# Graph layer on one core: the first four nodes' last 3456 edges counted instead of gathered

## The chip, the cores and the metric

The kernel runs on one core of a Trainium2 chip. TensorE (PE) multiplies, VectorE (DVE) and ScalarE (ACT) work elementwise, GpSimd (POOL) issues the indirect DMAs here (gathers and scatters by lists of rows), and SyncE (SP) and ACT issue plain DMAs. The metric is device time in microseconds, the median of several executions. The profile is of one execution.

## The reference

A layer on 3125 nodes with 256 features and 100000 edges, sorted by destination. `x` is normalized by rows; then the graph part, a linear-attention part and a mixture of experts follow:

```python
xn = _layernorm(x, axis=-1)
# graph part
e = relu((xn[dst] - xn[src]) @ theta_w.T + theta_b + xn[src] @ phi_w.T + phi_b)
gnn = segment_max(e, dst)              # 0 for a node without edges
# attention part: q, instance-normalized k and v, out = q (k^T v) / N, projected
x = x + gnn + mix(xn)
# experts: layernorm, router, two of eight experts (256 -> 1024 -> 256), weighted
x = x + ffn(_layernorm(x))
```

For a node d with edges, the maximum over edges of relu(a[d] + b[s]) is relu(a[d] + max b[s]), where a = xn theta^T + biases and b = xn (phi - theta)^T. So the graph part needs, for each node, the largest row b[s] over the sources s of its edges, feature by feature. An edge that occurs twice counts as once. The destinations are distributed as the square of a uniform number: low nodes have very many edges (node 0 has 1747), high nodes few.

## The kernel before

Nodes are cut into 25 tiles of 128 rows. Everything is done in the order of falling node numbers, so the edge lists are handed over reversed, with 96 filler edges (destination -1) at the end. 100096 edges are 782 columns of 128.

**Stages.** (1) All tiles are normalized, and b is computed and stored in DRAM as `b_d`. (2) The edges are worked through in four groups of columns, `GROUPS` and `STEPS` (lines 41 and 42): 240 columns for tiles 12 to 24, 161 for tiles 6 to 11, 228 for tiles 1 to 5, and 153 for tile 0 alone. One indirect DMA per column gathers 128 rows of `b_d` (line 1283, issued by the helper at line 102). Each of the 128 partitions holds a contiguous run of edges, so a running maximum along the columns, one DVE operation per column (`fold`, line 358), gives the maximum of every node that ends in the run; `cut` resets it where the destination changes. Windows of eight columns are stored to `s_d`. (3) When a group's columns are done, `carry` (line 361) passes maxima from one partition to the next with two transposes, a scan and two transposes back, and the tiles of the group are routed (`token_tile`, line 414): gather the last row of each node from `s_d`, add what is carried over, the linear parts, normalize, compute router scores, take the best two. `dispatch` scatters the tiles' rows into expert order (`xs_d`, line 109). (4) `Stream` (line 641) runs the experts for groups 0, 1 and 2 in units of 256 rows: first matmul (line 602), Gelu (line 604), second matmul (line 628), bias matmul (line 727); the results go to `ys_d`. (5) Tile 0, the last to be complete, isn't scattered: `dense_tile` (line 761) runs all eight experts on its 128 rows and weighs them. Its scaled inputs are made on DVE (line 777). (6) `combine` (line 1188) gathers each routed row's two results (48 gathers), weighs them (line 1201) and stores the output.

While the edges are gathered, the attention part (`mixer`, line 945) and the search for each node's last edge (`places`, line 282) run beside.

**What sets the order.** The order on PE, DVE, ACT and SP is the order in which the program writes the instructions (`manual_schedule`, line 828). A small planner in the program decides it: tasks are generators that yield how many ticks they wait; the clock `now` advances by one with each indirect DMA (lines 1010 to 1017 and 1284), and `on_pe` estimates PE's time so that the stream's steps are written as PE will need them. So a tick is about one POOL gather. A fold is written six ticks (`LAG`) after its gather, but for the very last columns, when no gather follows, at once (line 1246). DMAs on SP and ACT keep the order in which they are written. In this clock, group 1 is handed to the stream at tick 527; group 2's last fold is at tick 691, its scatters at 734 and 742, and it is handed over at 748; the edges end at 854, and the stream's end is estimated for 859.

**The end.** Group 3 (tile 0) begins its carry only when the stream has been written to its end:

```python
        while g == G - 1 and g - 1 not in at_hand["ffn"].through:
            yield 0.5
        start(carry(at_hand["tok"], mm, g, clock["last"], chain, carried))
```

The last six columns of group 3 aren't stored and gathered again, but picked by matmuls with one-hot columns (`pick_ends`, line 1176). Tile 0 uses ACT's Sqrt, then loads the Gelu table (line 465).

Before the end, `order` (line 895) checks that the edges are sorted and that each group holds only its nodes; if not, `verdict` sends the kernel to a general path behind line 1300, which doesn't run for these inputs.

## Time and profile before

| | |
|---|---|
| median of five runs | 1258.58 us (1247.89 to 1261.13) |
| the profiled execution | 1251.14 us, span 1249.1 us |
| busy: PE, DVE, ACT, POOL | 953.8, 651.1, 330.5, 910.2 us |
| edge gathers on POOL | 782, 762.0 us busy, 245.3 us idle before them |
| folds on DVE | 778, mean 484 ns |
| result gathers (`ys_d`) | 48 |
| last edge gather starts | 1148.0 us |
| stream's last matmul ends | 1150.2 us |
| dense tile, first to last matmul | 1171.6 to 1242.6 us |

The page shows one execution. Its slices cut the span into 40 parts of 31 us; a digit is a tenth of busy time. A group's line gives the busy time, the mean of one instruction, and the idle time of the engine before them with what ended most of it; "issue" is time in which nothing that the profile shows was waited for. In the timeline a row is start, duration, engine, line, operation, operands, and in brackets the wait before it.

### The profile page before, as it was taken

Reading aid. Unit: us, or ns where it says so; the run is one execution under the profiler, and the core shown is the slowest. Engines: PE = TensorE matmul, PEld = TensorE weight load, DVE = VectorE, ACT = ScalarE, POOL = GpSimd, SP = SyncE. Lnnn points to the kernel's source line nnn. Section 1 sums busy time; section 2 is a strip of 40 time slices with the busy share of each in tenths; the row PEclk is TensorE's granted clock in tenths of the full one; section 3 lists DMA queues with packets and bytes.
Section 4 is the critical chain, followed back from the end, with each engine's and each line's share of the span. In section 5 each row is a group of like instructions: output and inputs, shape, how many; then the busy total and the mean of one; then the engine's idle time right before and its main releaser. Section 6 shows DMA issues by size and latency. Waiting matters only on the chain.

```text
span 1249.1 us, 13251 instructions
## 1 busy us (share of the span) xinstructions
PE 953.8 (76%) x3894; PEld 686.9 (55%) x3894; DVE 651.1 (52%) x1931; ACT 330.5 (26%) x759; POOL 910.2 (73%) x938
## 2 busy tenths in 40 slices
PE   6548777739504469699999999999974449999777
PEld 5324333324202234288887888888862338886666
DVE  7668767863347663333348553333337833433632
ACT  4212222211101231133333333333310113332322
POOL 6677777777777777777777677777777777777751
PEclk9778988869855557799999999999995559999789
DMA  8669877676766654578877688999995669998581
GB/s 281 205 206 316 305 230 239 231 233 204 268 223 236 231 172 135 201 236 298 314 256 265 213 302 316 310 351 360 359 347 173 207 220 369 404 363 291 196 309 58
DMA packets 103276, 325.89 MB, mean 261 GB/s; under 512 B 20534, under 2 KB 41519, under 8 KB 91802
## 3 DMA queue, kind: packets, MB, share of 16 engines
q0 software_dynamic: 45328, 123.27, 32.0%
q1 hardware_dynamic: 26428, 115.34, 23.4%
q10 hardware_dynamic: 31438, 86.33, 19.6%
q8 instruction: 33, 0.54, 0.2%
q14 instruction: 49, 0.40, 0.1%
HBM read 192.97 MB, written 131.89 MB: 260 GB/s over the span
## 4 chain that ended last, share of the span: by engine, by line
PE 27%; DMA 25%; POOL 24%; issue 13%; DVE 10%; ACT 1%; POOLq 0%; DVEq 0%; SPq 0%; ACTq 0%
POOL g L102 23%; DMA g<-b_d,srcI 21%; PE hp L602 9%; PE yp L628 8%; DVE g L358 3%; DMA r<-s_d,end_i 2%; PE bp L234 2%; PE mm L395 2%; PE yp L727 1%; PE mm L393 1%; PE am L437 1%; POOL xs_d L109 1%; DVE r L442 1%; PE tr L227 1%; DVE r L443 1%
## 5 line engine op out<-in xcount | busy, mean ns | idle before, releaser
L102 POOL DMA_INDIRECT g<-b_d,srcI x782 | 762.0, 974 | 245.3 <-issue 214.2
L358 DVE SCALAR_TENSOR_TENSOR g<-g,cut 128x256 f32<-128x256 f32 x778 | 376.6, 484 | 425.0 <-DMA g<-b_d,srcI 409.9
L602 PE MATMUL hp<-xe,w 128*128 128x256 f32 (+1 forms) x1216 | 300.3, 373 | 12.0 <-issue 8.5
L628 PE MATMUL yp<-w,hT 128*128 128x256 f32 x1120 | 292.3, 383 | 0.0
L602 PEld LDWEIGHTS hp<-xe,w 128*128 128x128 f32 x1216 | 221.5, 195 | 51.5 <-issue 18.5
L604 ACT ACTIVATE hT<-hp,sm 128x256 f32<-128x256 f32 (+1 forms) x320 | 144.8, 453 | 336.2 <-PE hp L602 333.7
L628 PEld LDWEIGHTS yp<-w,hT 128*128 128x128 f32 x1120 | 207.5, 191 | 36.7 <-issue 11.0
L949 PE MATMUL kv<-wkv,xn_hi 128*128 128x512 f32 x104 | 60.8, 739 | 29.9 <-DVE kn L967 29.1
L949 PE MATMUL kv<-wkv,xn_lo 128*128 128x512 f32 x96 | 52.7, 700 | 36.7 <-DVE kn L967 22.6
L437 PE MATMUL am<-cr,oh 128*128 128x257 f32 x88 | 40.1, 590 | 42.9 <-DVE r L442 39.6
L102 POOL DMA_INDIRECT g<-ys_d,from_i x48 | 46.5, 968 | 27.4 <-issue 12.2
L949 PEld LDWEIGHTS kv<-wkv,xn_hi 128*128 128x128 f32 x104 | 23.5, 237 | 58.6 <-issue 52.7
L949 PEld LDWEIGHTS kv<-wkv,xn_lo 128*128 128x128 f32 x96 | 20.5, 225 | 61.3 <-issue 57.8
L437 PEld LDWEIGHTS am<-cr,oh 128*128 128x128 f32 x88 | 22.1, 284 | 52.8 <-issue 42.0
L727 PE MATMUL yp<-b_sb,ident 8*128 8x256 f32 x128 | 44.4, 426 | 0.0
L393 PE MATMUL mm<-bias,ones 1*128 1x512 f32 x50 | 31.8, 719 | 14.3 <-ACT x_sb L400 11.1
L953 ACT ACTIVATE sq<-kv 128x1024 f32<-128x1024 f32 x25 | 25.5, 1022 | 58.7 <-PE kv L949 58.7
L686 ACT ACTIVATE xe<-trf,sm 128x256 f32<-128x256 f32 x64 | 32.5, 561 | 21.3 <-PE trf L677 21.3
L972 PEld LDWEIGHTS dots_p<-kn,vn 128*128 128x128 f32 x200 | 26.8, 197 | 20.0 <-issue 20.0
L961 ACT ACTIVATE rsk<-var,eps 128x16 f32<-128x16 f32 x25 | 7.7, 308 | 110.0 <-DVE var L958 110.0
L109 POOL DMA_INDIRECT xs_d<-xn_hi,slot_i x26 | 27.1, 1043 | 9.9 <-issue 8.1
L972 PE MATMUL dots_p<-kn,vn 128*128 128x128 f32 x200 | 27.4, 282 | 8.7 <-DVE kn L967 8.7
(264 smaller groups left out, 947.5 us busy)
## 6 DMA issues: line engine op xcount, KB each, us to landing
s_d<-g SPq DMA_DIRECT2D x79, 1024.0 KB, 5.0
w<-in_w ACTq DMA_DIRECT2D x84, 512.0 KB, 7.0
s_d<-g SPq DMA_DIRECT2D x18, 896.0 KB, 4.3
g<-b_d,srcI POOLq DMA_INDIRECT x782, 4.3
w<-in_w ACTq DMA_DIRECT2D x6, 2048.0 KB, 9.6
xn_hi<-xs_d ACTq DMA_DIRECT2D x16, 512.0 KB, 4.5
xs_d<-zero ACTq DMA_DIRECT2D x8, 512.0 KB, 6.3
xs_d<-zero ACTq DMA_DIRECT2D x16, 256.0 KB, 3.3
```

The source lines that it names most:

```text
L102: got = nc.gpsimd.indirect_dma_start(out=to, out_offset=None, in_=table, in_offset=row_index(index))
L109: put.append(nc.gpsimd.indirect_dma_start(out=table, out_offset=row_index(index), in_=of, in_offset=None))
L358: nc.vector.scalar_tensor_tensor(g[:, j, :], last, cut[:, t:t + 1], g[:, j, :], op0=OP.add, op1=OP.max)
L393: nc.tensor.matmul(am, ones[0:1, :], bias, start=True, stop=False)
L437: nc.tensor.matmul(r2, picks[k], carried[g], start=(k == 0), stop=(k == len(slices) - 1))
L602: nc.tensor.matmul(hp[:, 0:n], w1t[:, c, f, :], xe[:, c, 0:n], start=(c == 0), stop=(c == 1))
L604: nc.scalar.activation(hT[f][:, 0:n], hp[:, 0:n], AF.Gelu, bias=sm[:, 4 + f, e:e + 1])
L628: nc.tensor.matmul(yp[r], hT[q][:, r * P:(r + 1) * P], w2t[:, q, :], start=(q == 0), stop=(q == FC - 1 and self.whole))
L686: nc.scalar.activation(xe[:, c, :], self.held["tr", u][:, c, :], AF.Identity, bias=sm[:, 2 + c, e:e + 1], scale=sm[:, c, e:e + 1])
L727: nc.tensor.matmul(yp, ident[0:E, e:e + 1].to_broadcast([E, P]), b2_sb, start=False, stop=True)
L949: nc.tensor.matmul(kv[:, k, :], xnT(i, c), wkv[:, c, k * INNER:(k + 1) * INNER], start=(c == 0), stop=(c == 1))
L972: nc.tensor.matmul(dots_p[:, r, :], vn[:, r * P:(r + 1) * P], knf[:, r * P:(r + 1) * P], start=(i == 0 and r == 0), stop=(i == NT - 1), sk ...
```

## The change

The last 27 columns (3456 edges, 96 of them filler) are taken out of group 3, which has 126 columns left; they belong to nodes 0 to 3 alone. For these columns `first_nodes` counts, by bf16 matmuls of one-hot matrices, how often each of the 3125 nodes is a source of an edge to each of the four nodes, and turns the counts into a mask: 0 where there is an edge, -1e38 where there is none. It is written early, between `borders` and `places`. `first_maxima` then reads the whole of `b_d` again, one 128x256 tile after the other on SP's queue, and takes for each of the four nodes max(b + mask) on DVE: 100 operations of 128x256, one per two ticks, begun when group 1 is handed to the stream. Transposes and a reduction bring the maximum over the partitions; tile 0's routing takes it in with one more maximum on four rows.

Further: the carry of group 3 no longer waits until the stream is written to its end; instead the dense tile waits for that after its transposes and before its first scaling. Tile 0 takes its roots on DVE (`newton=True`) instead of by ACT's Sqrt, and two table loads are dropped. The indices of the 27 columns are loaded by two DMAs of their own, the sortedness check knows a fifth slice, and a last edge beyond the gathered columns now gives "no row" instead of the last gathered row.

```diff
-STEPS = (240, 161, 228, 153)
+STEPS = (240, 161, 228, 126)
+FIRST = 4
+REST = T - COL[G]
...
-            nc.vector.tensor_scalar(end_i[:, i0:i1], has[:, i0:i1], float(most), None, op0=OP.min)
+            nc.vector.scalar_tensor_tensor(end_i[:, i0:i1], has[:, i0:i1], float(most), has[:, i0:i1], op0=OP.is_le,
+                                           op1=OP.mult)
...
             nc.vector.tensor_max(r1, r1, also["rows"])
+            nc.vector.tensor_max(r1[0:FIRST, :], r1[0:FIRST, :], also["first"])
...
         if then:
-            nc.scalar.activation(table, eps, AF.Gelu)
...
             clock["through"] = True
-            nc.scalar.activation(table, eps, AF.Sqrt)
...
+        while ready is not None and "through" not in ready:
+            yield 1
         scaled(0)
...
-        while ready is not None and "through" not in ready:
-            yield 1
         units = Units(ps, act, P, True)
...
-    for g in range(G):
-        move(nc.sync, srcI[:, COL[g]:COL[g + 1]], rows_of(src, g))
-        move(nc.sync, dstI[:, COL[g]:COL[g + 1]], rows_of(dst, g))
+    for g in range(G + 1):
+        of_slice = slice(COL[g], COL[g + 1] if g < G else T)
+        move(nc.sync, srcI[:, of_slice], rows_of(src, g))
+        move(nc.sync, dstI[:, of_slice], rows_of(dst, g))
...
         yield from borders(ea, mm, firsts, lasts, ok, following)
+        yield 4
+        yield from first_nodes()
         yield 80
         yield from places(ea, mm, run, keys, [(GROUPS[g], P * COL[g + 1]) for g in range(G)], following)
+    def first_nodes():
...
+        counts = no_edge.rearrange("p k i -> p (k i)")
+        some = 7
+        for t0 in range(0, REST, some):
+            n = min(some, REST - t0)
+            ones_of = []
+            for name, at, width in (("lanes", low, P), ("tiles", high, FIRST * NT)):
+                ones_of.append(ea.tile([P, some, width], BF16, name=name))
+                nc.vector.tensor_tensor(ones_of[-1][:, 0:n, :], apart[:, None, 0:width].to_broadcast([P, n, width]),
+                                        at[:, t0:t0 + n, None].to_broadcast([P, n, width]), OP.is_equal)
+                yield 2
+            count_p = mm.tile([P, FIRST * NT], F32, name="mm")
+            for t in range(n):
+                nc.tensor.matmul(count_p, ones_of[0][:, t, :], ones_of[1][:, t, :], start=(t == 0), stop=(t == n - 1))
+            yield 3
...
+        nc.vector.tensor_scalar(counts, counts, 0.5, NEG, op0=OP.is_lt, op1=OP.mult)
...
-        while g == G - 1 and g - 1 not in at_hand["ffn"].through:
-            yield 0.5
         start(carry(at_hand["tok"], mm, g, clock["last"], chain, carried))
...
-                              then=lambda: start(dense), also=ends))
+                              newton=True, then=lambda: start(dense), also=ends))
...
+        if g == 1:
+            start(first_maxima())
...
+    def first_maxima():
+
+        i0 = GROUPS[1][0]
+        of_k = xn_lo[:, i0:i0 + FIRST, :]
+        b_rows = b_d.rearrange("(i p) d -> p i d", p=P)
+
+        def bring(i):
+            if i < NT:
+                move(nc.sync, xn_lo[:, SPLIT - 2 + i % 2, :], b_rows[:, i, :])
+
+        bring(0)
+        yield 8
+        for i in range(NT):
+            bring(i + 1)
+            b = xn_lo[:, SPLIT - 2 + i % 2, :]
+            for k in range(FIRST):
+                if i == 0:
+                    nc.vector.tensor_scalar(of_k[:, k, :], b, no_edge[:, k, 0:1], None, op0=OP.add)
+                else:
+                    nc.vector.scalar_tensor_tensor(of_k[:, k, :], b, no_edge[:, k, i:i + 1], of_k[:, k, :], op0=OP.add,
+                                                   op1=OP.max)
+                yield 2
+        most = at_hand["first"].tile([P, 2, FIRST], F32, name="most")
+        for c in range(2):
+            tr = mm.tile([P, FIRST, P], F32, name="mm")
+            for k in range(FIRST):
+                nc.tensor.transpose(tr[:, k, :], of_k[:, k, c * P:(c + 1) * P], ident)
+            on_pe(1.2)
+            yield 4
+            nc.vector.tensor_reduce(most[:, c, :], tr, AX.X, OP.max)
+            yield 2
+        rows_p = mm.tile([FIRST, 2, P], F32, name="mm")
+        for c in range(2):
+            nc.tensor.transpose(rows_p[:, c, :], most[:, c, :], ident)
...
-                    while clock["edges"] < min(COL[g] + t0 + j + LAG, T):
+                    while clock["edges"] < min(COL[g] + t0 + j + LAG, COL[G]):
```

## The prediction

> **What bounds the kernel now.** First the page's slices, then the table of stretches, then the time order of the last 100 us.
>
> ```profile
> PE   6548777739504469699999999999974449999777
> ...
> POOL 6677777777777777777777677777777777777751
> ...
> PEclk9778988869855557799999999999995559999789
> ...
> L102 POOL DMA_INDIRECT g<-b_d,srcI x782 | 762.0, 974 | 245.3 <-issue 214.2
> ```
>
> POOL is evenly busy from the first gather to slice 37: one gather each 1.29 us (762.0 + 245.3 over 782) and almost no waits. PE is full in slices 17 to 29 (expert stream, groups 0 and 1), drops for three slices at half clock, is full again (group 2), and thins out. So POOL bounds up to group 2's last gather (945 us); then comes group 2's routing, then its 131 us of PE work; beside that work run group 3's gathers; then tile 0.
>
> ```profile
> 951.00:1003.00 52.00, 24.06 (x74) 18.41 (x74) 45.37 (x215) 7.59 (x17) 39.06 (x41) 0.50 0.54 182
> 1018.00:1150.00 132.00, 131.19 (x586) 106.70 (x585) 50.73 (x113) 43.24 (x95) 99.97 (x104) 0.97 0.95 350
> 1150.20:1171.60 21.40, 11.92 (x35) 7.30 (x34) 9.11 (x32) 4.88 (x9) 16.22 (x18) 0.68 0.72 258
> 1171.60:1242.70 71.10, 61.98 (x387) 56.44 (x387) 31.06 (x83) 23.63 (x65) 30.89 (x32) 0.91 0.56 194
> ```
>
> Columns: stretch, length, busy time of PE, weight load, DVE, ACT, POOL, then clock, DMA share, GB/s. In group 2's routing (951 to 1003) DVE is 87% busy: it is the engine on the path. During the stream PE has no gap. After it come 21.4 us in which PE only serves tile 0's routing, then 71 us of dense tile.
>
> ```profile
> 1109.66 0.69 PE L727 MATMUL yp<-b_sb,ident 8*128 8x256 f32 x2
> 1110.28 1.13 PE L602 MATMUL hp<-xe,w 128*128 128x256 f32 x4
> ...
> 1156.35 0.48 DVE L358 SCALAR_TENSOR_TENSOR g<-g,cut 128x256 f32<-128x256 f32 x1 [0.36 <-DMA g<-b_d,srcI]
> ...
> 1171.64 6.44 PE L602 MATMUL hp<-xe,w 128*128 128x128 f32 x36 [1.12 <-DVE xe L777]
> ```
>
> The stream's last matmul ends at 1150.2 and the last fold at 1156.8: the two strands end almost together. **Both** must end before tile 0, so shortening one alone gives at most the 6.6 us between them, unless tile 0's routing can be done inside the other. The change does allow that.
>
> **The change, part by part.** *27 gathers fewer on POOL.* The last 27 start 1.265 us apart (1113.86 to 1148.01), so 34.2 us go. The last one would start at 1113.9, land at 1120.7 (as the one there does) and be folded by 1121.4. The stream isn't shortened by that; it becomes the only bound.
>
> *Tile 0's routing moves into the stream.* Without the wait on the stream's end (L1072) and with the dense tile waiting only before its first scaling, the 21.4 us between stream and dense tile close: **-21.4**. Three things come back on PE, whose instructions run in the written order:
> - Tile 0's own matmuls: 11.9 us busy in the gap at clock 0.68, so 11.9 x 0.68 = 8.1 us at the stream's full clock: **+8.1**.
> - A wait for the last fold. The planner's clock counts one tick per indirect DMA; in the kernel before, the edges end at tick 854 and expert unit 30 is written from tick 826. 27 gathers fewer, they end at 827, and the last folds and the carry's transposes (L365) are written there without the usual lag of 6 ticks, after one step of unit 30. PE reaches that place 1.72 us after 1110.28, at 1112.0; the fold is ready at 1121.4: **+9.4** (bounds 6, with the 4 us less that an early landing gives, and 11, with the landings of 8.6 us that the last gathers have now). Everything behind the transposes waits: the rest of units 30 and 31.
> - After a pause of that length PE is slow. After the 8.5 us pause at 1206.7 the next five pieces took 1.19, 0.85, 0.85, 0.85 and 0.61 us where 0.44 is usual: **+2.2**. Further hand-overs of tile 0 (six between PE, DVE and ACT) mostly have a few microseconds of stream steps written between; I take **+2** (0 to 6).
>
> The Gelu table load (1.28 + 0.20 us) and the Sqrt in tile 0's chain go, and twelve small DVE operations of 0.16 to 0.23 us come: 2.4 us, beside the stream, where DVE is idle 60%. Uncovered they would cost 1 us net.
>
> *100 maxima on DVE.* Nearest row: the fold, 484 ns alone, 0.41 apart in a dense run. They start 8 ticks after group 1 goes to the stream (tick 527) at one in 2 ticks: ticks 535 to 733. From 745 to 945 us DVE has folds worth 75.8 us in 200, so the first 78 hide. But group 2's last fold is at tick 691 and its scatters at 734 and 742, so 22 maxima are written inside group 2's routing. Those before tick 702 fall into waits for the row gather (2.6 us) and its neighbours; the 15 at ticks 702 to 731 lengthen a full DVE queue, and POOL's scatter waits behind it, with all later gathers, and the stream behind both: 15 x 0.42 = **+6.3** (3 if DVE's small gaps take half; 12 if the two reductions from PSUM and the transposes that feed them, at ticks 735 to 747, also hold up the second half's slots).
>
> A rule to weigh here. In that same stretch POOL's gathers keep their 946 ns and 0.30 us gaps although DVE is 87% busy. The Trainium skill, "SBUF — State Buffer", section "SBUF: two separate sides", says that DVE instructions in two-port modes lock POOL out of a shared port, so that it can't write its descriptors; at its harshest that would put 100 x 0.48 = 48 us on POOL. The row shows nothing of it, and the sum takes zero.
>
> *Loads and stores.* 25 loads of 128 KB join SP's queue, each written 8 ticks (10 us) before use, against landings of 4 to 7 us. Each waits for the maxima of two tiles before, and group 3's stores stand behind it; five windows of eight columns are slack enough for 6 us. 27 columns of gathers and stores (3.4 MB each) go. Two more index loads cost SP 0.8 us at most, ahead of the first gather, which waits for b_d anyway. Taken as nothing.
>
> *The counts, early.* Eight comparisons of 600 to 896 elements (nearest rows: 692 ns for 512, 969 for 781) are 8.5 us, with the short ones about 11 us of DVE and 27 small matmuls, around 100 to 140 us, where DVE is 75% busy; the search for the nodes' last edges moves 33 ticks later and still ends (tick 194) before group 0's (245). POOL waits for none of it. Zero; uncovered, 11.
>
> *The dense tile.* Its 71.0 us contain a pause that looks like a late weight load but isn't:
>
> ```profile
> 1205.80 0.95 POOL L102 DMA_INDIRECT g<-ys_d,from_i  x1 [8.44 <-DVE g L1201]
> ...
> 1211.48 0.48 DVE L1201 SCALAR_TENSOR_TENSOR g<-g,share,x_sb 128x256 f32<-128x256 f32 x1 [6.04 <-DMA g<-ys_d,from_i]
> ...
> 1214.76 0.60 DVE L777 TENSOR_SCALAR xe<-xT,sm 128x128 f32<-128x128 f32 x2
> ...
> 1215.20 1.19 PE L602 MATMUL hp<-xe,w 128*128 128x128 f32 x4 [8.53 <-issue]
> ```
>
> PE waits for the scaled input of the sixth expert (L777), which stands in DVE's queue behind combinations (L1201), which wait for result rows, whose gathers waited for a buffer held by an output store that took 15.6 us beside three weight loads of 2 MB. After the change the combinations of groups 0 and 1 run some 25 us earlier against the dense tile, before those weight loads: **-8.5** and its slow pieces **-2.2**. The first 36 matmuls (6.44 us) follow a full-clock stream: 36 x 0.11 = 4.0, **-2.4**. New is that group 2's result rows can only be gathered after the stream: store 7 us, eight gathers 10 us, landing 3 to 7, so 20 to 24 us after its end; the fifth expert's input stands behind them and is needed after 3.5 + 3 x 7.0 = 24.5 us. I take **+2** (0 to 8).
>
> **Sum.** -21.4 + 8.1 + 9.4 + 2.2 + 2 + 6.3 - 8.5 - 2.2 - 2.4 + 2 = -4.5 us. The profiled execution took 1251.1 (span 1249.1); that gives 1246.6. It was 7.4 us below the median of the five runs, 1258.6, which the forecast goes by: 1254.
>
> **Rivals.** *Faster:* the hand-overs fit. The fold lands early (6 instead of 9.4), the small waits are none, DVE's gaps swallow half of the maxima (3 instead of 6.3), no new wait in the dense tile: -4.5 - 3.4 - 2 - 3.3 - 2 = -15, 1243. For it: DVE is only 38% busy in the stream, and the dense tile loses its worst wait. Against it: the lag is missing just where PE is ahead.
>
> *Slower: the vector queue during group 2's routing.* Place: ticks 691 to 747. Price: every added microsecond there delays scatter, stream and end one for one. With 12 for the maxima, reductions and transposes and an 8 us wait in the dense tile the sum is -4.5 + 5.7 + 6 = +7, 1266. It decides from 11 us of delay in that stretch (6.3 + 4.5). For it: 87% busy. Against it: the second half's slots have 3.4 us of slack today (done near 1003, used from 1006.4).
>
> *The pause stays:* the dense tile again waits 8.5 + 2.2 us for an input behind combinations: -4.5 + 8.7 = +4, 1263; it needs group 1's combinations to slip by 15 us.
>
> *The change doesn't apply:* the verdict (L1298) would send the kernel to its general path if a node above 3 were among the last 3456 edges. By the inputs 3587 edges go to nodes 0 to 3 and 3360 are needed, so it can't.
>
> **How the numbers follow.** Forecast 0.45, faster rival 0.27, slower rival 0.15, staying pause 0.13. A measurement of this kernel tells about 1% (12.6 us) from no change. All of these lie within some 15 us of zero, so: faster by over 1% 0.29 (most of the faster rival and a little of the forecast's lower edge), within 1% 0.56, slower 0.15 (the two upper cases with both bounds together). Range: the lower bounds of all terms add to -17, the upper ones to +12 and a little more, on 1258.6: 1239 to 1271.
>
> **What would show it.** Right: the last edge gather some 28 us earlier; a PE pause of 6 to 11 us before L365 inside unit 30; dense matmuls right behind the last L727; group 2's first scatter about 6 us later; no pause before the sixth expert. Wrong: a POOL wait of over 11 us at L109, no pause at L365, or a dense tile that still takes 70 us.

## The result and the profile after

The changed kernel takes 1256.9 us (median of 52 runs, 1246.1 to 1266.0); the kernel before takes 1252.6 us (median of 94 runs, 1246.1 to 1263.3). Run beside each other they stand at a ratio of **1.0021**, 95% interval [1.0009, 1.0034]: some 2.6 us slower. The forecast was 4.5 us faster. Both are within 1% of no change, and 1256.9 lies in the range, but the sign of the sum was wrong.

The profiled execution of the changed kernel took 1258.0 us (span 1256.2; before 1249.1). That is more than the ratio says, and the reason is found below.

From the page of the changed kernel, busy tenths in 40 slices, the granted clock, and the group of edge gathers (busy us, mean ns, idle before them):

```profile
PE   6547776637813569699999999999983539996997
...
POOL 6677777777777776677777777777777767776530
...
PEclk9778889858955565899999899999995559898999
...
L106 POOL DMA_INDIRECT g<-b_d,srcI x755 | 739.3, 979 | 238.4 <-issue 199.2
```

27 gathers are gone (755 for 782), and one takes 979 ns at the mean where it took 974. PE's thin slices after group 2's stream are gone too; there is one slice at 6 instead, inside the stream.

Three stretches of the changed kernel, in the columns of the prediction (length, then busy time of PE, weight load, DVE, ACT, POOL, then clock, DMA share, GB/s): group 2's routing, its stream from the first to the last matmul, and the dense tile.

```profile
951.00:1016.00 65.00, 29.15 (x87) 21.03 (x87) 56.10 (x246) 7.58 (x17) 46.78 (x48) 0.53 0.51 166
1031.70:1189.10 157.40, 144.98 (x620) 116.77 (x620) 64.40 (x171) 44.01 (x98) 107.34 (x112) 0.93 0.84 300
1189.20:1248.30 59.10, 58.28 (x387) 53.21 (x386) 14.88 (x39) 23.68 (x65) 13.63 (x14) 1.00 0.55 193
```

The stream starts at 1031.7 instead of 1018.8 (+12.9) and takes 157.4 us instead of 131.4 (+26.0). The 21.4 us behind it are down to 0.1 (-21.3). The dense tile takes 59.0 us instead of 71.0 (-12.0), all of it at full clock. Together +5.6.

The stream's two waits, from the time order of the changed kernel (start, duration, engine, instruction, and in brackets the idle time before it and what ended it):

```profile
1130.77 0.48 DVE L365 SCALAR_TENSOR_TENSOR g<-g,cut 128x256 f32<-128x256 f32 x1 [1.08 <-DMA g<-b_d,srcI]
...
1136.28 0.48 DVE L365 SCALAR_TENSOR_TENSOR g<-g,cut 128x256 f32<-128x256 f32 x1 [5.02 <-DMA g<-b_d,srcI]
...
1136.82 0.69 PE L372 MATMUL mm<-ident,g 128*128 128x128 f32 x2 [6.26 <-DVE g L365]
...
1158.97 0.60 ACT L471 ACTIVATE xt<-x_sb,off,root 128x256 f32<-128x256 f32 x1 [2.99 <-DVE off L469]
...
1159.62 0.44 PE L482 MATMUL mm<-ident,xt 128*128 128x128 f32 x2 [4.26 <-ACT xt L471]
```

The first is the one that I had forecast: the carry's transposes (L372) are written too early and wait for the last fold, 6.26 us with the rest of units 30 and 31 behind them. The second is tile 0's chain on VectorE (sum, normalization, three Newton steps), for which too few expert steps are written in between. The end of the stream and the start of the dense tile, on PE:

```profile
1188.38 0.69 PE L734 MATMUL yp<-b_sb,ident 8*128 8x256 f32 x2
1189.01 1.16 PE L609 MATMUL hp<-xe,w 128*128 128x128 f32 x8
1190.90 4.22 PE L609 MATMUL hp<-xe,w 128*128 128x128 f32 x28 [0.73 <-ACT hT L611]
```

The dense matmuls follow the last L734 without a gap, and the first 36 take 6.1 us from start to end of which 0.7 is a wait (6.4 before, at a granted clock of 0.75). The pause before the sixth expert is gone, and no new wait for the fifth came.

Two things stay open after the comparison: why the stream starts 12.9 us later where the maxima were to cost 6.3, and whether tile 0's routing is worth having in the stream at all, at 26.0 us for a gap of 21.3.

### The profile page after: what moved, and what is told of

It reads as the page before. It is cut to its first block, busy times and chain, and to the rows that moved or that the text cites. A ratio compares the mean times of both kernels' runs of the same rounds, so it can differ in the third digit from the quotient of the medians.

```text
span 1256.2 us, 13411 instructions
## 1 busy us (share of the span) xinstructions
PE 966.0 (77%) x3931; PEld 694.3 (55%) x3931; DVE 685.3 (55%) x2039; ACT 326.9 (26%) x754; POOL 887.8 (71%) x911
## 3 DMA queue, kind: packets, MB, share of 16 engines
q1 hardware_dynamic: 29740, 115.08, 23.5%
## 4 chain that ended last, share of the span: by engine, by line
PE 36%; DMA 27%; POOL 16%; DVE 10%; issue 10%; ACT 1%; ACTq 0%; POOLq 0%; DVEq 0%; SPq 0%
DMA g<-b_d,srcI 22%; POOL g L106 15%; PE hp L609 13%; PE yp L635 12%; DVE g L365 4%; PE mm L402 2%; PE yp L734 2%; DMA w<-in_w 2%; PE bp L240 1%; PE mm L400 1%; DMA r<-s_d,end_i 1%; DMA b_d<-bt 1%; PE trf L684 1%; DMA xn_lo<-b_d 1%; PE am L445 1%
## 5 line engine op out<-in xcount | busy, mean ns | idle before, releaser
L106 POOL DMA_INDIRECT g<-b_d,srcI x755 | 739.3, 979 | 238.4 <-issue 199.2
L365 DVE SCALAR_TENSOR_TENSOR g<-g,cut 128x256 f32<-128x256 f32 x751 | 363.1, 484 | 370.2 <-DMA g<-b_d,srcI 354.2
L609 PE MATMUL hp<-xe,w 128*128 128x256 f32 (+1 forms) x1216 | 300.0, 372 | 2.7 <-ACT xe L693 1.7
L609 PEld LDWEIGHTS hp<-xe,w 128*128 128x128 f32 x1216 | 220.3, 194 | 42.0 <-issue 10.3
L1206 DVE SCALAR_TENSOR_TENSOR xn_lo<-xn_lo,no_edge 128x256 f32<-128x256 f32 x96 | 46.0, 479 | 0.6 <-DMA xn_lo<-b_d 0.6
L400 PE MATMUL mm<-bias,ones 1*128 1x512 f32 x50 | 34.7, 779 | 14.1 <-ACT x_sb L407 10.8
L734 PE MATMUL yp<-b_sb,ident 8*128 8x256 f32 x128 | 44.9, 430 | 0.0
L113 POOL DMA_INDIRECT xs_d<-xn_hi,slot_i x26 | 26.9, 1037 | 14.8 <-issue 13.6
```

Source lines behind the costliest of these rows:

```text
L106: got = nc.gpsimd.indirect_dma_start(out=to, out_offset=None, in_=table, in_offset=row_index(index))
L365: nc.vector.scalar_tensor_tensor(g[:, j, :], last, cut[:, t:t + 1], g[:, j, :], op0=OP.add, op1=OP.max)
L400: nc.tensor.matmul(am, ones[0:1, :], bias, start=True, stop=False)
L609: nc.tensor.matmul(hp[:, 0:n], w1t[:, c, f, :], xe[:, c, 0:n], start=(c == 0), stop=(c == 1))
L734: nc.tensor.matmul(yp, ident[0:E, e:e + 1].to_broadcast([E, P]), b2_sb, start=False, stop=True)
L1206: nc.vector.scalar_tensor_tensor(of_k[:, k, :], b, no_edge[:, k, i:i + 1], of_k[:, k, :], op0=OP.add, op1=OP.max)
```

## The experiments

All ratios are to the kernel before, from runs beside it. Lines are those of the changed kernel unless a kernel is named.

### The new order alone

The kernel before, with all its gathers, in the new order of tile 0's work.

```diff
-        while g == G - 1 and g - 1 not in at_hand["ffn"].through:
-            yield 0.5
...
+        while ready is not None and "through" not in ready:
+            yield 1
         scaled(0)
...
-            nc.scalar.activation(table, eps, AF.Gelu)
...
-            nc.scalar.activation(table, eps, AF.Sqrt)
...
+                              newton=True, then=lambda: start(dense), also=ends))
```

> The kernel before with all its 782 gathers, no counts and no maxima; only the order of tile 0's work is that of the changed kernel (no wait for the stream's end, the wait ahead of the first scaling, no table loads). Theory (the schedule can gain only where the last fold comes well before the stream's end): here the last fold is ready at about 1157 us, after the stream, so tile 0's routing still stands behind the stream; 13 to 20 us stay between the last stream matmul and the first dense one, and the time is 1 to 5 us under that of before. Rival (the new order itself is the gain, the fewer gathers are not needed): the 21 us gap closes to under 8 and the time falls by 10 or more.

Measured: 1257.7 us, ratio **1.0029** [1.0010, 1.0048]. Both expectations missed: the order alone is a small loss. Its stretches, the stream, what lies behind it, and the dense tile:

```profile
1023.70:1169.80 146.10, 136.71 (x599) 110.53 (x599) 53.56 (x121) 42.36 (x94) 110.69 (x115) 0.95 0.92 337
1169.80:1182.60 12.80, 5.00 (x20) 3.73 (x21) 7.60 (x31) 1.82 (x4) 9.75 (x11) 0.79 0.68 226
1182.60:1253.30 70.70, 63.30 (x388) 58.12 (x388) 31.29 (x84) 23.62 (x65) 27.12 (x28) 0.89 0.54 188
```

The gap shrinks by 8.6 us, but the stream grows by 14.7: its last part now stands behind the carry's transposes, which wait 6.37 us for the last fold. The dense tile keeps its pause (7.38 us), since the result rows come no sooner. So moving the routing doesn't pay while the edges end behind the stream. With 27 gathers fewer the same order gains, as the next run shows.

### Without counts and maxima

Nodes 0 to 3 lack their last 3456 edges in the result.

```diff
-        yield 4
-        yield from first_nodes()
...
-        bring(0)
-        yield 8
-        for i in range(NT):
...
+        nc.vector.memset(ends["first"], NEG)
```

> The changed kernel without the counts and without the maxima; the last 3456 edges of nodes 0 to 3 are left out of the result. Theory (the counting delays group 2's routing; some of the delay in the one profile was the clock's chance): the first stream matmul of group 2 comes 5 to 9 us sooner than in the changed kernel (1031.7), the time is 5 to 9 us under the changed kernel's, so 2 to 7 under that of before. Rival A (the whole 12.9 us are the counting's): 12 to 14 us under the changed kernel. Rival B (they are the clock's chance): within 2 us of it.

Measured: 1248.2 us, ratio **0.9950** [0.9926, 0.9974]. So everything but the counting is worth -6.3 us, and counts and maxima together cost 0.71% or **8.9 us** (some 3.5 us either way). The first matmul of group 2's stream comes at 1019.4, 12.3 us sooner than in the changed kernel. The theory holds by the time (5 to 9 us), rival A by the one profile (12 to 14). 3.1 of the 12.3 us are a wait of another kind, 7.21 us against 4.15, which comes below under "Group 0's second scatter". Two rows of its trace, the stream and ten microseconds after the wait for tile 0's scaled rows:

```profile
1019.40:1182.30 162.90, 148.41 (x620) 118.73 (x620) 64.60 (x171) 43.97 (x98) 107.66 (x111) 0.90 0.81 290
...
1148.00:1158.00 10.00, 9.38 (x26) 7.04 (x27) 1.70 (x10) 1.97 (x5) 5.77 (x7) 0.50 0.42 129
```

With the same number of matmuls (620) the stream takes 162.9 us here and 157.4 in the changed kernel. The wait ahead of L372 is 7.75 us here, and after the second wait the clock stays at half for ten microseconds: four matmuls of L609 take 1.91 us there (at 1149.5) where they take 1.03 in the rows of the next run. PE's busy time in the stream is 148.4 us here, 17 over the kernel before, where the sum had put 10.3 for tile 0's matmuls and the slow ones.

### The last folds spread

```diff
                         yield 1
+                    if COL[g] + t0 + j > COL[G] - LAG:
+                        yield 1
                     last = fold(wins[g, w], j, COL[g] + t0 + j, last)
...
-    start(finale())
+    start(finale(), clock["now"] + LAG)
```

> The changed kernel, with the last six folds written one in each tick after the last gather, so that the carry's transposes stand five ticks later in TensorE's order, and the result rows' gathers start six ticks later. Theory (6.3 us of the stream's 26 are a wait for the last fold, because the transposes are written too early): the wait ahead of L372 falls from 6.26 us to under 1, and the time by 4 to 7 us against the changed kernel. Rival (TensorE would wait in the next hand-over instead, for the row gather or for the scaled rows of tile 0): the other waits of the stream grow by 4 us or more together and the time stays within 2 us.

Measured: 1249.1 us, ratio **0.9954** [0.9928, 0.9980], 0.67% or 8.4 us under the changed kernel. The theory holds in kind; the gain lies above its 4 to 7 us, but is known only to some 3.6 us either way. On PE there is no wait ahead of the transposes; the picks of the last rows (L1262) and expert steps surround them:

```profile
1130.31 0.59 PE L1262 MATMUL am<-g,xn_lo 128*128 128x256 f32 x2
1130.74 0.38 PE L372 MATMUL mm<-ident,g 128*128 128x128 f32 x2
1130.96 0.60 PE L1262 MATMUL am<-g,xn_lo 128*128 128x256 f32 x2
1131.39 1.03 PE L609 MATMUL hp<-xe,w 128*128 128x256 f32 x4
```

Its stream and its dense tile:

```profile
1025.80:1173.60 147.80, 142.87 (x620) 115.33 (x620) 61.20 (x165) 43.93 (x99) 100.91 (x105) 0.95 0.85 309
1173.70:1237.20 63.50, 60.22 (x387) 54.52 (x387) 17.52 (x46) 23.74 (x65) 20.08 (x21) 0.97 0.54 202
```

The stream is 9.6 us shorter than in the changed kernel: 7.5 of idle time (157.4 - 145.0 against 147.8 - 142.9) and 2.1 of matmul time, at a clock of 0.95 for 0.93. The wait for the scaled rows is shorter too (2.48). Some of it comes back: the dense tile takes 4.4 us more, with a wait of 2.42 us for the sixth expert's input, behind combinations that now come later. The rival had put that into the stream; it is in the dense tile, and about half as large as the 9.6 us.

### The old wait

The carry of group 3 waits for the stream's written end again; the counting stays.

```diff
+        if g == G - 1:
+            r_first = last_rows(at_hand["tok"], 0, rows)
+            while g - 1 not in at_hand["ffn"].through:
+                yield 0.5
         start(carry(at_hand["tok"], mm, g, clock["last"], chain, carried))
...
-    start(finale())
+    start(finale(), clock["now"] + 26)
```

> The changed kernel, with group 3's carry waiting for the written end of the expert stream, as in the kernel before (the row gather of tile 0 stays where it is, and the result rows' gathers start 26 ticks later, about where the kernel before has them). Theory (what tile 0 costs inside the stream, 26 us, is more than the gap that it closes, 21): the stream from the first to the last matmul of group 2 takes 131 to 134 us again, 18 to 22 us stand behind it, and the time is 0 to 5 us under the changed kernel's if the dense tile keeps its 57 us. Rival (the routing inside the stream is what the change gains): 8 us or more above the changed kernel.

Measured: 1271.8 us, ratio **1.0139** [1.0113, 1.0166], 14.8 us over the changed kernel. My theory fell, the rival holds.

```profile
1035.30:1180.10 144.80, 137.75 (x598) 109.74 (x598) 40.71 (x95) 43.03 (x95) 90.51 (x93) 0.96 0.82 299
1180.10:1190.80 10.70, 3.75 (x17) 2.50 (x16) 7.28 (x31) 0.97 (x2) 7.80 (x8) 0.84 0.68 233
1190.80:1268.10 77.30, 67.11 (x393) 60.97 (x393) 31.02 (x85) 23.90 (x66) 23.26 (x24) 0.87 0.48 165
```

Stream, gap and dense tile are 232.8 us against 216.5 in the changed kernel. The comparison of 26 us in the stream with 21 us of gap was too narrow: the third row is the larger part. The dense tile takes 77.3 us instead of 59.1, with these pauses on PE:

```profile
1226.17 1.19 PE L609 MATMUL hp<-xe,xn_lo 128*128 128x128 f32 x4 [3.75 <-DVE xe L783]
...
1241.29 0.98 PE L609 MATMUL hp<-xe,w 128*128 128x128 f32 x3 [5.12 <-issue]
```

In the new order the combinations of groups 0 and 1 are done against the stream's end, and the dense tile's inputs (L783) no longer stand behind them. That is the pause that the prediction took out of the sum (-8.5 and -2.2). The stream doesn't return to 131 us either, because the picks of the last rows still wait in it for folds (2.40, 1.20 and 0.71 us ahead of L1262). As the result rows' gathers start later as well, this run shows the two together, not the carry's place alone.

### The maxima sooner

```diff
                                                    op1=OP.max)
-                yield 2
+                yield 1.5
```

> The changed kernel with one maximum in 1.5 ticks in place of 2, so that the last is written at tick 685, before group 2's routing (691); a second execution, since the first fell on a chip where the kernel before took 1820 us. Theory (part of the maxima's cost is their place in VectorE's queue during that routing): the wait ahead of group 2's first scatter falls from 4.2 us to under 1.5 and the ratio from the changed kernel's 1.0021 to 0.999 to 1.0005. Rival (their cost is only that gathers beside them are slower): ratio 1.001 to 1.003. My prediction's term would give 0.997.

Measured: 1253.8 us, ratio **0.9992** [0.9965, 1.0018], some 3.6 us under the changed kernel, with an interval that allows nearly nothing or twice that. The wait ahead of group 2's first scatter on POOL, first in the changed kernel:

```profile
1009.07 1.24 POOL L113 DMA_INDIRECT xs_d<-xn_lo,slot_i  x1 [4.20 <-issue]
```

and with the maxima sooner:

```profile
995.56 1.00 POOL L113 DMA_INDIRECT xs_d<-xn_lo,slot_i  x1 [0.30 <-issue]
```

The theory holds: the wait is gone and the ratio lies in its range. So the term of the prediction is likely real and within its bounds (3.6 by the time, against 6.3 with bounds of 3 and 12). But it isn't all of the 8.9 us.

### Three edits together

The last folds spread, the maxima sooner, and up to two ticks instead of one between tile 0's steps (the third edit is shown).

```diff
-            return min(ticks, 1) if at_once else ticks
+            return min(ticks, 2) if at_once else ticks
```

> The changed kernel with the last folds spread, the maxima sooner, and up to two ticks in place of one between tile 0's steps; a second execution, since the first fell on a chip where the kernel before took 1820 us. Theory (each of the three waits is a loss of its own): ratio 0.991 to 0.993 against 0.9954 with spread folds alone, and no wait of over 1.5 us in group 2's stream. Rival (what is saved in the stream comes back in the dense tile): ratio 0.994 to 0.997, and waits of 5 us or more in the dense tile.

Measured: 1245.4 us, ratio **0.9937** [0.9913, 0.9961]: faster than the kernel before by 7.9 us and than the changed kernel by 10.5. Its stream and its dense tile:

```profile
1023.00:1166.20 143.20, 140.74 (x619) 114.05 (x619) 55.84 (x151) 43.82 (x99) 98.27 (x101) 0.96 0.86 310
1166.60:1231.40 64.80, 61.64 (x387) 55.73 (x387) 22.71 (x57) 23.44 (x64) 23.29 (x24) 0.95 0.63 218
```

The waits of 6.26 and 4.26 us are gone from the stream (L482 follows the expert steps at once), and it takes 143.2 us. Part of it comes back, as the rival had it: the dense tile is 5.7 us longer than in the changed kernel, here with a wait for the fourth expert's input, written behind a combination (L1283) that waits for a gather:

```profile
1188.45 0.48 DVE L1283 SCALAR_TENSOR_TENSOR g<-g,share 128x256 f32<-128x256 f32 x1 [5.75 <-DMA g<-ys_d,from_i]
...
1189.25 0.59 DVE L783 TENSOR_SCALAR xe<-xT,sm 128x128 f32<-128x128 f32 x2
...
1189.68 1.19 PE L609 MATMUL hp<-xe,g 128*128 128x128 f32 x4 [2.93 <-issue]
```

The ratio lies between the two expectations, a little under the rival's lower end, and its interval overlaps that of the spread folds alone (0.9954). That it beats the kernel before is shown; that it beats the spread folds is not.

### Group 0's second scatter

In the profiles so far one wait varied without a reason in the code: POOL's standstill ahead of group 0's second scatter, at about 500 us. Between the last gather and that scatter in the changed kernel:

```profile
497.98 0.94 POOL L106 DMA_INDIRECT g<-b_d,srcI  x1 [0.30 <-issue]
506.13 1.01 POOL L113 DMA_INDIRECT xs_d<-xn_hi,slot_i  x1 [7.21 <-issue]
```

and with the last folds spread, a kernel with the same instructions up to there:

```profile
499.43 1.10 POOL L106 DMA_INDIRECT g<-b_d,srcI  x1 [0.30 <-issue]
500.84 1.01 POOL L113 DMA_INDIRECT xs_d<-xn_hi,slot_i  x1 [0.30 <-issue]
```

The wait beside the clock granted to PE from 480 to 500 us, in the eight profiles whose order of instructions is the same there (before and the kernels named above):

| kernel | clock, 480 to 500 us | wait, us |
|---|---|---|
| old wait | 0.50 | 11.65 |
| changed | 0.54 | 7.21 |
| new order alone | 0.55 | 7.03 |
| three edits | 0.86 | 1.19 |
| before | 0.87 | 2.30 |
| no counts, no maxima | 0.96 | 4.15 |
| folds spread | 0.96 | 0.30 |
| maxima sooner | 1.00 | 0.30 |

In that stretch PE works off the edge-free parts of tiles 0 to 11 (L400 to L403), and the small matmul that the scatter's slots need (L526) stands behind them; VectorE waited for it some 22 us in the changed kernel and 12.8 with the folds spread. PE was full in all eight (19.64 to 20.00 of the 20 us), but got through 25 to 49 matmuls. First the changed kernel, then the one with the folds spread:

```profile
480.00:500.00 20.00, 19.64 (x29) 7.50 (x28) 0.28 (x2) 2.58 (x8) 14.36 (x16) 0.54 0.37 103
480.00:500.00 20.00, 19.64 (x49) 8.29 (x48) 6.77 (x30) 3.52 (x12) 15.12 (x17) 0.96 0.40 123
```

At half clock the same matmuls take about twice as long: four of L402 took 3.78 us at 488.8 in the changed kernel and 1.98 at 501.1. The kernel without counting (0.96 and 4.15 us) falls out of the series because its POOL arrives some 3 us sooner at the same event. So up to 11 us of an execution go with the clock there in kernels of this order, and a single profile of each can't tell a change of a few microseconds. Why the clock differs isn't seen.

An edit to take that chance away moves those matmuls behind the second scatter:

```diff
-        if g == 0:
-            start(rest_without_edges())
         while any(t[2] is one for t in tasks for one in waiting):
             yield 1
         yield 5
+        if g == 0:
+            start(rest_without_edges())
```

> The changed kernel with the edge-free part of tiles 0 to 11 written after group 0's last scatter; a second execution, since the first fell on a chip where the kernel before took 1820 us; there this kernel was slower than the kernel before (ratio 1.018) although its wait ahead of the second scatter was 4.8 us against 23 to 29 in three others. Theory (the scatter waits for a small matmul behind those groups, and the clock decides how long): the wait falls to under 2.5 us, group 2's stream starts 2 to 7 us sooner, ratio 0.997 to 1.0005. Rival (the moved matmuls delay the first stream or group 1's routing by as much or more): the start of group 2's stream is not sooner, ratio 1.001 to 1.02.

Measured: 1268.1 us, ratio **1.0103** [1.0069, 1.0136]. The wait did fall to 0.30 us, and the scatter stood at 501.1 for 506.1. But group 2's stream starts at 1040.0, 8.3 us later than in the changed kernel: the rival holds. Two stretches of this kernel, around the start of group 2's routing:

```profile
920.00:946.00 26.00, 26.00 (x119) 21.35 (x118) 14.72 (x34) 9.10 (x20) 19.90 (x21) 1.00 1.00 360
946.00:960.00 14.00, 14.00 (x64) 11.28 (x63) 2.01 (x5) 3.59 (x8) 5.71 (x6) 1.00 0.97 366
```

and the same stretches of the changed kernel:

```profile
920.00:946.00 26.00, 16.40 (x70) 12.34 (x68) 14.83 (x34) 3.38 (x8) 19.91 (x21) 0.86 0.94 355
946.00:960.00 14.00, 7.17 (x16) 4.17 (x16) 9.38 (x28) 0.00 (x0) 10.65 (x12) 0.50 0.69 218
```

PE had been free from 936 us on, with 9.9 us to spare before group 2's carry. With the moved matmuls in front, group 1's stream still fills it at 946 to 960, and the carry, then everything behind it, waits. The slack of an engine is what is left before the next chain needs it, and here it was smaller than the work that I put there.

With the three edits together the same step takes back their gain:

> The kernel with three edits (last folds spread, maxima sooner, up to two ticks between tile 0's steps) and the edge-free part of tiles 0 to 11 written after group 0's last scatter. If both theories hold, the gains add: 2 to 5 us under the kernel with three edits, ratio 0.987 to 0.991. If the moved matmuls delay what follows: no faster than the kernel with three edits.

Measured: 1254.6 us, ratio 0.9996 [0.9974, 1.0018], 0.59% or 7.4 us over the three edits without it (0.82% or 10.3 us in the changed kernel). The moved matmuls delay what follows in both.

### How counts and maxima divide

The counts alone were to settle it, and two other forms of their comparisons. The second of them:

```diff
-                nc.vector.tensor_tensor(ones_of[-1][:, 0:n, :], apart[:, None, 0:width].to_broadcast([P, n, width]),
-                                        at[:, t0:t0 + n, None].to_broadcast([P, n, width]), OP.is_equal)
+                for t in range(n):
+                    nc.vector.tensor_scalar(ones_of[-1][:, t, :], apart[:, 0:width], at[:, t0 + t:t0 + t + 1], None,
+                                            op0=OP.is_equal)
```

(The first, by column, keeps the comparison of two tiles, one column in each instruction.)

> The changed kernel with the counts and without the maxima; the last 3456 edges of nodes 0 to 3 are left out of the result (a further execution, since the earlier ones fell on chips where the kernel before took some 1820 us). Without both the ratio is 0.995, with both 1.0021, with maxima sooner 0.9992. Theory (the counts cost some 2.5 us through slower gathers beside them): ratio 0.9965 to 0.998. Rival A (the counts cost nothing on the path): 0.994 to 0.996. Rival B (the counts are the larger part): 0.9985 or more.

> The changed kernel with each wide comparison of the counts (7 columns of 128 or 100, two inputs in SBUF, 0.78 to 1.09 us) made as seven of one column each, same kind. Theory (a gather is held for as long as one such instruction runs): no gather between 100 and 120 us takes over 1.3 us, the mean from 95 to 150 us falls from 1.056 to under 1.01 us; the time moves by -2 to +2 us (the short ones take more VectorE time). Rival (it is the sum of VectorE's work that slows the gathers): the mean stays at 1.03 us or more.

> The changed kernel with the same comparisons column by column, against one number per partition in place of a second tile. Theory (it is the kind with two tiles that holds the gathers up): gathers of 95 to 150 us at the mean of the kernel without counts, 0.98 us, none over 1.25, and no slower as a whole than with one-column comparisons of two tiles. Rival (any comparison does it): as with two tiles by column.

> The changed kernel unaltered, a second profile. Theory (the wait ahead of group 0's second scatter, 7.2 us in the first profile, is set by the granted clock of that execution): another value between 0.3 and 11.7 us, with the granted clock from 480 to 500 us above 0.75 where it is under 2.5 and under 0.65 where it is over 5. Start of group 2's stream less that wait: 1021 to 1024 us, as in the first profile (1022.7). Rival (the wait belongs to the change): 6 to 8 us again.

> The kernel with three edits (last folds spread, maxima sooner, up to two ticks between tile 0's steps; ratio 0.9937) with the counts' comparisons made column by column against one number per partition. On the slow chips gathers beside these took 0.99 us at the mean against 1.03 to 1.07 beside the wide ones. Theory (the counts' cost is slower gathers): mean of the gathers from 95 to 150 us under 1.01 against 1.05, ratio 0.991 to 0.993. Rival (the 54 short comparisons take more VectorE time, in a stage where it is 75% busy, and cost as much): ratio 0.9935 or more.

These fell on chips where the kernel before took 1820 to 1852 us, so their times don't decide the question: counts alone 0.9896 [0.9846, 0.9947] (0.9843 and 0.9868 in two other executions), by column 0.9846 [0.9791, 0.9902], by scalar 0.9842 [0.9776, 0.9907], three edits with the scalar form 0.9799 [0.9745, 0.9853], the changed kernel itself 1793.4 us in its one execution beside 1836.0. On such chips first executions of three kernels gave 0.9816 (maxima sooner), 0.9845 (three edits) and 1.0178 (edge-free parts later). What differs is seen in POOL's waits of the kernel with counts alone (total, times, longest, in us):

```profile
POOL g L106 <- DMA s_d<-g: 259.0, 14, 50.4
```

The gathers wait for window buffers that the stores of folded rows hold. In the changed kernel's first profile the edge gathers have no wait of that kind among those of over 1 us in total. That the 27 gathers and stores fewer are what gains 1 to 2% there is likely but not shown. What else was using the memory there isn't seen; the page calls a third of the chain "another core or an unknown queue".

The profiles from these chips do answer what was asked of the gathers. The comparisons run there from about 150 us on, so the stretches named in the expectations miss most of them. Of the gathers that overlap the time from the first to the last comparison, the mean and the longest are 1.09 to 1.16 and 1.61 to 1.78 us with the wide comparisons (seven profiles), 1.07 and 1.98 by column, and 0.99 and 1.18 to 1.19 against one number per partition (two profiles). So the comparisons of two tiles slow the gathers, and cutting them into columns helps little (the gather of 1.98 us stands beside seven comparisons in a row): the theory of the form by column fell, its rival holds, and the theory of the scalar form holds for the gathers. What the scalar form is worth in time on the other chips isn't measured. The second profile of the changed kernel has a wait of 22.3 us ahead of group 0's second scatter, which comes at 652 us there, so it decides nothing about the clock from 480 to 500 us.

What remains to divide the 8.9 us are the eight profiles above. POOL's order is the same in each, so the time from one indirect DMA to another shows what lies between. In us, with the wait of the table above taken off where a stretch holds it (numbers of indirect DMAs from the program's start, the first being no. 0):

| kernel | start of no. 100 | no. 559 to 720 | 720 to 758 | 758 to 775 | stream's first matmul, less the wait |
|---|---|---|---|---|---|
| before | 146.0 | 205.8 | 48.0 | 22.3 | 1016.5 |
| new order alone | 146.9 | 205.2 | 48.7 | 21.8 | 1016.6 |
| no counts, no maxima | 146.4 | 205.3 | 48.8 | 23.5 | 1015.2 |
| changed | 149.2 | 207.3 | 49.7 | 26.1 | 1024.5 |
| folds spread | 149.3 | 208.2 | 50.3 | 24.8 | 1025.6 |
| old wait | 147.2 | 207.7 | 49.8 | 26.1 | 1023.7 |
| maxima sooner | 148.9 | 204.7 | 48.5 | 22.7 | 1018.4 |
| three edits | 149.7 | 207.6 | 48.7 | 23.7 | 1021.9 |

With the wait taken off, the last column falls into two groups: 1016.1 at the mean without counting and **1024.6** with it, 8.5 us later, and the three of each group within 2 us. That agrees with the 8.9 us of the times. It divides so:

- **Counts:** +2.1 us up to no. 100 in the three kernels with counts and with the maxima at their place (+2.4 over all five with counts), of which 1.7 are left at no. 373 (498.0 against 496.3 us). The gathers beside the wide comparisons are slower. In the changed kernel, on VectorE:

```profile
100.78 1.09 DVE L965 TENSOR_TENSOR lanes<-apart,of_lane 128x896 bf16<-128x896 f32 x1
...
108.11 1.08 DVE L965 TENSOR_TENSOR lanes<-apart,of_lane 128x896 bf16<-128x896 f32 x1
```

and on POOL at those times:

```profile
101.02 1.66 POOL L106 DMA_INDIRECT g<-b_d,srcI  x1 [0.30 <-DMA g<-b_d,srcI]
...
108.17 1.84 POOL L106 DMA_INDIRECT g<-b_d,srcI  x1 [0.30 <-issue]
```

- **Gathers beside the maxima** (no. 559 to 720): +2.3 us in the same three. It lies in the gathers themselves: those of this stretch take 983 to 988 ns at the mean in the three, 970 to 973 without counting, with the same idle time between them (49.3 to 49.4 us). In the changed kernel the 37 gathers that a maximum overlaps longest take 1039 ns, and those with no VectorE instruction beside them 947. With the maxima sooner the share is nothing in one kernel (966 ns) and 2.2 in the other (984), so it is the least certain.
- **The maxima in group 2's routing** (720 to 775): 1.4 + 3.1 = 4.5 us in those three, 0.8 on average where they are sooner. This is the prediction's 6.3. The shares come from one profile of each kernel; no run shows the times of counts and maxima apart.

## Why the prediction was wrong

The sum against what was measured, in us:

| step | forecast | measured |
|---|---|---|
| gap between stream and dense tile | -21.4 | -21.3 |
| tile 0's matmuls and the half clock after pauses | +8.1 +2.2 | +13.8 |
| wait for the last fold | +9.4 | +6.3 |
| further hand-overs | +2 | +5.9 |
| counting, ahead of the stream | +6.3 | +8.5 |
| dense tile | -11.1 | -12.0 |
| sum | -4.5 | +1.2 |

The measured sum agrees with the ratio's +2.6 (1.1 to 4.3). Of the 5.7 us between the two sums, the stream makes 4.3 and the counting 2.2; the dense tile gives back 0.9. The two profiled spans differ by 7.1 us: the wait ahead of group 0's second scatter (7.21 against 2.30) makes 4.9 of that, and 1.4 stand behind the dense tile's last matmul.

**Right.** The mechanism of each large step: 21 us of gap close; the carry's transposes wait for the last fold inside unit 30, because the lag is missing there; the pause before the sixth expert was combinations ahead of its input and goes; the dense tile runs behind a stream at full clock. The dense tile's gain needs the new order (77.3 us with the old wait and the later result gathers) and the fewer gathers (70.7 us with the order alone). Two of the signs were off: the last edge gather came 20.5 us earlier (1127.6 against 1148.0), not 28, and group 2's first scatter 13.1 us later, not 6; 4.9 of these 13.1 are the wait ahead of group 0's second scatter.

**The step that failed most: what tile 0's routing costs inside the stream.** The sum had 8.1 + 9.4 + 2.2 + 2 = 21.7 us, and 26.0 were measured. The wait for the fold came out smaller (6.3 for 9.4; 5.1 to 9.5 in other profiles). The slow matmuls behind the pauses (+2.2) and the further hand-overs (+2) were sized too small. PE's busy time rose by 13.8 us (145.0 against 131.2) where 10.3 were put down, at a clock of 0.93 over the stretch instead of 0.98. Busy time times clock gives an estimate of how it divides: some 6 us for tile 0's matmuls, where 8.1 were put, and some 7.5 for the slower clock, where 2.2 were. The hand-overs were 5.9 for 2: 4.26 for the scaled rows alone. I had taken "a few microseconds of stream steps written between", while the code gives tile 0's steps one tick each; the chain from tile 0's sum to the scaled rows is 5.9 us on VectorE and ScalarE (1153.67 to 1159.57), and a tick is one gather, 1.25 us. Spreading the folds took away the first wait and the time followed (0.9954). Spreading tile 0's steps as well took away the second; that this gains time of its own isn't shown (0.9937).

**"POOL's gathers keep their 946 ns" was read in the wrong stretch.** The sum took zero for slower gathers, from group 2's routing, where VectorE is 87% busy with short operations; even there 946 is the median of the 31 gathers and 954 the mean. The page had the other answer in the line that the prediction itself shows: a mean of 974 ns over 782 gathers. Paired with the VectorE instruction that overlapped it longest, a gather of the kernel before took 981 ns at the mean beside a fold, which reads two tiles in SBUF, and 947 with none beside it. Its longest gather, at the program's start, stands beside a wide subtraction of two tiles:

```profile
55.13 2.29 DVE L943 TENSOR_TENSOR wkv<-wkv,wm 128x2048 f32<-128x2048 f32 x1
...
55.70 2.54 POOL L102 DMA_INDIRECT g<-b_d,srcI  x1 [0.30 <-issue]
```

The comparisons of the counts are of that kind, with two tiles. By the stretches above the counts and the maxima cost 1.7 and 2.3 us in this way, 4.0 where the sum had nothing. The Trainium skill, "SBUF — State Buffer", section "SBUF: two separate sides", states an exclusive lock on a shared port; the direction agrees with these rows (gathers of 1.66 and 1.84 us beside comparisons of 1.09 and 1.08). The prediction's harshest reading of it, 48 us for the 100 maxima, doesn't agree with the 2.3.

**The counts, "Zero".** POOL doesn't wait for the counts, which was my reason; it is slowed beside them, which I hadn't asked.

**The maxima through VectorE's queue** were forecast at 6.3 within 3 and 12, and cost 4.5 by the stretches; placing them sooner won 3.6 by the time. That term lies within its bounds, and the slower rival, which hung on it, was rightly placed but not reached: it needed 11 us of delay there, and there were 4.5.

**Luck, and a slip.** The forecast time, 1254, is 2.9 us from the measured 1256.9 by luck: it starts from five runs whose median was 6.0 us above that of the 94, and the fold's wait and the maxima, put too high by 3.1 and 1.8 us, made up for part of what was missing. The range's lower end doesn't follow from its terms: their lower bounds add to -15.2, not -17, and -17 on 1258.6 is 1242, not 1239.

## What to carry to other kernels

When work is moved into a stream that bounds, price each hand-over twice, as the wait that is left in the written order and as the slow matmuls behind it, and write the consumer as many ticks after its producer as the chain between them takes. Look for what a gather costs beside the kind of instruction that is added, not beside a busy engine. Before a gap of a few microseconds between two profiles is explained, find the waits that vary between executions of the same instructions and take them off. In the profile of before, look at the longest single instructions beside the kind that is added, not at the mean alone.

## What was not expected of the hardware

- The clock granted to PE at one place (480 to 500 us) was between 0.50 and 1.00 in executions of the same instructions there, and one wait behind it between 0.3 and 11.65 us, 0.9% of the kernel's time.
- After the wait for the scaled rows the clock stayed at 0.50 over the ten microseconds from 1148 in one execution, though PE was busy for 9.38 of them.
- Gathers from 100 to 122 us, first in the changed kernel, with the counts' comparisons beside them (instructions, busy us, mean ns, idle before them):

```profile
L106 POOL DMA_INDIRECT g<-b_d,srcI x16 | 18.4, 1152 | 4.9 <-issue 3.4 <-DMA g<-b_d,srcI 0.6 <-DVE kn L1010 0.3
```

and in the kernel before:

```profile
L102 POOL DMA_INDIRECT g<-b_d,srcI x18 | 18.3, 1015 | 5.5 <-issue 5.2 <-DVE both L965 0.3
```

- In three of five series of runs the kernel before took 1820 to 1852 us instead of 1253, with the same program, on other chips. There the kernel with the maxima sooner stood at a ratio of 0.982 for 0.999 and the one with three edits at 0.985 for 0.994; the changed kernel itself has only one execution there, 1793.4 us beside 1836.0.
